# Two rows of a sample per partition in the stores, products in two column tiles, residual inside the matrices

## The chip, the cores and the metric

The kernel runs on one core of a Trainium2 chip. The metric is the device time of one execution in microseconds (us). The core has a matrix engine (TensorE, PE in the profile, with its weight loads listed as PEld), a vector engine (VectorE, DVE), a scalar engine (ScalarE, ACT), GpSimd (POOL) and a sync engine (SyncE, SP). Here ACT and SP only issue transfers, which 16 DMA engines carry out. Matmul results land in a separate memory, PSUM; everything else is in SBUF, a memory of 128 partitions.

## The reference

`x` holds 128 samples of 128 x 1024 f32 values. Each sample has a subject, 0 to 7, and each subject a 128 x 128 matrix. The output is the sample plus the product with its subject's matrix:

```
def _L0_cond_ref(x, subjects, weights):
    w = weights[subjects]
    out = jnp.einsum('bct,bcd->bdt', x, w)
    return out
x = x + _L0_cond_ref(x, itok_B_0_7, L0_cond_weights)
```

The input and the output are 67.11 MB each, the matrices 0.52 MB.

## The kernel before

The 128 samples are worked in `NT` = 32 groups of four. A slot of SBUF holds one group, and there are `SLOTS` = 12 slots. A slot takes the group's input, is added to in place, and is stored from; so a slot is loaded again only when its store has landed (`s_slot`, L222).

**Loads** (`load`, L134, loop at L218) are issued on ACT's queue, one per sample. In DRAM a load reads runs of 16 KB (`ROWS` = 4 rows), in SBUF it writes 4 KB per partition.

**Stores** (`store`, L142, loop at L247) are issued on SP's queue, one per group, and one per two groups for the last 12. SBUF has one row of a sample per partition, so a store writes runs of 4 KB in DRAM. It reads 16 KB runs in SBUF, and 32 KB runs for the last `WHOLE` = 6 groups, where two groups lie next to each other. The first store (L251) is issued in another form, with 4 KB on both sides. From group `EARLY` = 8 on, until the last `LAST` = 8, a store waits until `BEHIND` = 4 more groups have been added (L249).

**Matrices.** The weights arrive over SP's queue (L192) and are sorted by two transposes on DVE and 16 copies on DVE and GpSimd (L208 to L239). For each sample, `place` (L163) copies the subject's matrix from `w_all` to one of four working matrices.

**PE** (`multiply`, L168) runs a loop over the groups in two halves of two samples. A sample takes two matmuls of 512 columns, which the profile records as two each. The two halves of PSUM (`ps`) are filled in turn.

**DVE** (`add`, L183) adds PSUM to the slot in place, half a group per instruction, then places the matrices of the next group.

Semaphores tie them together: GpSimd passes on `s_ready` to PE when a group's loads have landed, `s_go` says that matrices are placed, `s_product` that a half of PSUM is full, `s_added` that a half group is ready for its store. The last store is issued outside the block, after all engines have left it.

Of the kernel before, what the change touches and what calls it, by code (L numbers as in the profile page):

```python
# [25 lines left out]
F32 = mybir.dt.float32  # L26
I32 = mybir.dt.int32
ALU = mybir.AluOpType


G = 2
H = 2

N = 512

SLOTS = 12

P_SLOTS = 2

BEHIND = 4  # L40

EARLY = 8
LAST = 8

PAIR = 2
WHOLE = 6

DMA = 16

SORTED = 18  # L50

IDLE = 3

ROWS = 4

# [25 lines left out]
def kernel(  # L81
# [7 lines left out]
    nc = tc.nc  # L89
    B, C, T = x.shape  # L90
    S, _, D = weights.shape
    NT = B // (G * H)

    def sbuf(name, *shape, dtype=F32):
        return ctx.enter_context(nc.sbuf_tensor(name, list(shape), dtype)).ap()


    room = -(nc.sbuf_base + -nc.sbuf_base % 32) % ALIGN
    if room:
        sbuf("room", C, room // 4)  # L100
    x_all = sbuf("x_all", C, SLOTS * H * G * T)
    xs = [
        x_all[:, i * H * G * T : (i + 1) * H * G * T].rearrange("c (q t) -> c q t", t=T)
        for i in range(SLOTS)
    ]
    w_all = sbuf("w_all", C, S, D)
    w_raw, w_mid, w_late = (xs[SLOTS - 1][:, q, :] for q in range(3))
    ws = [sbuf(f"w{i}", C, 1, D) for i in range(H * G)]
    zeros = sbuf("zeros", C, N)
    given, near, wrap = (sbuf(name, 1, B, dtype=I32) for name in ("given", "near", "wrap"))  # L110
    index = sbuf("index", 1, B + H * G, dtype=I32)
    ps = [
        ctx.enter_context(nc.psum_tensor(f"ps{i}", [D, G, T], F32)).ap() for i in range(P_SLOTS)
    ]
# [4 lines left out]
    s_zeros = tc.alloc_semaphore("s_zeros")  # L119
    s_product = tc.alloc_semaphore("s_product")  # L120
    s_added = tc.alloc_semaphore("s_added")

    s_ready = tc.alloc_semaphore("s_ready")
    s_go = tc.alloc_semaphore("s_go")

    s_slot = [tc.alloc_semaphore(f"s_slot{k}") for k in range(SLOTS)]
    s_head = tc.alloc_semaphore("s_head")
    s_sort = tc.alloc_semaphore("s_sort")

    def emptied(i):  # L130
        turns = i // SLOTS
        return DMA * (H * G + 1) * turns - (DMA * G if i >= SLOTS and i % SLOTS == 0 else 0)

    def load(engine, i, q):  # L134
        transfer(
            nc,
            engine,
            xs[i % SLOTS][:, q, :],
            x[i * H * G + q].rearrange("(a r) t -> a (r t)", r=ROWS),
        ).then_inc(s_head if i * H * G + q < G else s_slot[i % SLOTS], DMA)  # L140

    def store(i, n):  # L142
        at = i % SLOTS * H * G * T
# [9 lines left out]
    def subjects_of(i):  # L153
        _, subject = nc.values_load_multi_w_load_instructions(
            index[0:1, i] if isinstance(i, slice) else index[0:1, bass.ds(i * (H * G), H * G)],
            engines=[mybir.EngineType.DVE],
            min_val=0,
            max_val=S - 1,
            skip_runtime_bounds_check_because="the index is clamped on the chip above",
        )  # L160
        return subject

    def place(h, subject):  # L163
        for q in range(h * G, (h + 1) * G):
            copy = nc.vector.tensor_copy(ws[q], w_all[:, bass.ds(subject[q], 1), :])  # L165
        copy.then_inc(s_go, 1)

    def multiply(slot, h):  # L168
        nc.tensor.wait_ge(s_go, 1).then_inc(s_go, -1)
        nc.tensor.wait_ge(s_ready, 1).then_inc(s_ready, -1)  # L170
        for q in range(h * G, (h + 1) * G):
            for t in range(0, T, N):
                at = slot * (H * G * T) + (q * T + t)
                mm = nc.tensor.matmul(  # L174
                    ps[h][:, q % G, t : t + N],
                    ws[q][:, 0, :],
                    x_all[:, bass.ds(at, N)],
                    start=True,
                    stop=True,
                )  # L180
        mm.then_inc(s_product, 1)

    def add(slot, h):  # L183
        mine = x_all[:, bass.ds(slot * (H * G * T) + h * G * T, G * T)]
        nc.vector.wait_ge(s_product, 1).then_inc(s_product, -1)  # L185
        nc.vector.tensor_tensor(  # L186
            mine, ps[h].rearrange("d g t -> d (g t)"), mine, ALU.add
        ).then_inc(s_added, 1)

    with tc.tile_critical():  # L190

        nc.sync.dma_start(  # L192
            w_raw, weights.rearrange("s (u j) d -> (s u) (j d)", j=S)
        ).then_inc(s_wall, DMA)
        nc.sync.dma_start(given, subjects.rearrange("(o b) -> o b", o=1)).then_inc(s_given, DMA)

        nc.vector.memset(zeros, 0.0).then_inc(s_zeros, 1)  # L197
        nc.tensor.wait_ge(s_zeros, 1)
        for _ in range(IDLE):
            nc.tensor.matmul(  # L200
                ps[P_SLOTS - 1][:, G - 1, :N], zeros[:, :D], zeros, start=True, stop=True
            )

        nc.vector.wait_ge(s_wall, DMA)
        nc.vector.transpose(  # L208
            w_mid.rearrange("p (e h w j) -> p j h e w", e=S, h=4, w=4), w_raw
        ).then_inc(s_sort, 1)  # L210
        nc.vector.memset(index[:, B:], 0).then_inc(s_index, 1)  # L211
        nc.vector.wait_ge(s_given, DMA)
        nc.vector.tensor_scalar(near, given, -S, S - 1, ALU.max, ALU.min).then_inc(s_index, 1)  # L213
        nc.vector.wait_ge(s_index, 2)
        nc.vector.tensor_scalar(wrap, near, 0, S, ALU.is_lt, ALU.mult).then_inc(s_index, 1)  # L215
        nc.vector.wait_ge(s_index, 3)
        nc.vector.tensor_tensor(index[:, :B], near, wrap, ALU.add).then_inc(s_index, 1)  # L217
        for i in range(NT):  # L218
            if i == SLOTS - 1:
                nc.scalar.wait_ge(s_sort, SORTED)  # L220
            if i >= SLOTS:
                nc.scalar.wait_ge(s_slot[i % SLOTS], emptied(i))  # L222
            for q in range(H * G):
                load(nc.scalar, i, q)

        nc.vector.wait_ge(s_sort, 1)
        nc.vector.transpose(w_late, w_mid).then_inc(s_sort, 1)  # L227

        def sort(engine, o, v):
            engine.tensor_copy(  # L230
                w_all[32 * v : 32 * (v + 1), 2 * o : 2 * (o + 1), :],
                w_late[32 * o : 32 * (o + 1)].rearrange("c (e v d) -> c v e d", v=4, d=D)[:, v],
            ).then_inc(s_sort, 1)

        nc.vector.wait_ge(s_sort, 2)
        nc.gpsimd.wait_ge(s_sort, 2)
        for o in range(4):
            for v in range(4):
                sort(nc.gpsimd if v == 3 else nc.vector, o, v)  # L239
        for i in range(NT):  # L240
            if i == 0:
                nc.gpsimd.wait_ge(s_head, DMA * G).then_inc(s_ready, 1)
                nc.gpsimd.wait_ge(s_slot[0], DMA * G).then_inc(s_ready, 1)
            else:
                nc.gpsimd.wait_ge(s_slot[i % SLOTS], emptied(i) + DMA * H * G).then_inc(s_ready, H)

        for i in [*range(NT - SLOTS), *range(NT - SLOTS, NT, PAIR)]:  # L247
            n = 1 if i < NT - SLOTS else PAIR
            nc.sync.wait_ge(s_added, (i + n + (BEHIND if EARLY <= i < NT - LAST else 0)) * H)  # L249
            if i == 0:  # L250
                nc.sync.dma_start(  # L251
                    out[: H * G].rearrange("g d t -> d g t"), xs[0]
                ).then_inc(s_slot[0], DMA)
            elif i + n < NT:
                store(i, n).then_inc(s_slot[i % SLOTS], DMA)


        nc.vector.wait_ge(s_index, 4)
        nc.vector.wait_ge(s_sort, SORTED)
        subject = subjects_of(slice(0, H * G))  # L260
        for h in range(H):
            place(h, subject)
        with nc.vector.Fori(0, NT) as turn:  # L263
            subject = subjects_of(turn + 1)
            for h in range(H):
                add(turn % SLOTS, h)
                place(h, subject)
        with nc.tensor.Fori(0, NT) as turn:
            for h in range(H):
                multiply(turn % SLOTS, h)  # L270

    with tc.tile_critical() as waits:
        for i in range(NT - SLOTS, NT - PAIR, PAIR):
            nc.scalar.wait_ge(s_slot[i % SLOTS], emptied(i + SLOTS))
    last = store(NT - PAIR, PAIR)

    tc.add_manual_dep(
        last.ins,
# [31 lines left out]
```

## Time and profile before

| What | Value |
|---|---|
| Median of 3 runs (lowest to highest) | 323.02 us (322.99 to 323.08) |
| Profiled execution: span of the instructions | 320.9 us |
| Between the span and the runs' median | 2.1 us |
| HBM read, written | 67.63 MB, 67.11 MB |
| Load of one sample, median from issue to landing | 34.2 us |
| Store of one group, median from issue to landing | 18.3 us |
| Store of two groups, median from issue to landing | 30.3 us |

The profile lists for each engine its busy time, and, in 40 equal slices of the span, the busy share of each engine and of the DMA engines. A group row gives line, engine, operation, output and inputs, then the count, the busy time with the mean duration of one, and the idle time before them with what ended it. A queue row gives packets, megabytes and the time that the packets took as a share of 16 engines over the window asked for; q10 carries the loads of x here, and q1 the stores and the matrices. A timeline row gives start, duration, and what was run how often, and in brackets the wait ahead of it.

### The profile page before, as it was taken

The page shows a single profiled execution, that of the slowest core. Times are in us where ns is not written, and L with a number is a line of the kernel's source. Part 1 is how long each engine was busy: PE and PEld are TensorE (multiplying, and loading weights), DVE is VectorE, ACT ScalarE, POOL GpSimd, SP SyncE. Part 2 cuts the span into 40 slices and gives each one's busy share as a digit, 9 for nine tenths or more (in the row PEclk, how much of TensorE's full clock was granted, in tenths as well). Part 3 has the DMA queues.
Part 4 walks back from the last instruction along what each step waited for, and adds up shares of the span by engine and source line. Part 5 has one row for each costly group of instructions (what it writes and reads, how often), then busy time and mean ns, then how long its engine had stood idle before and what let it go on. Part 6 is the DMA issues. An engine that isn't in the chain of part 4 may idle for free. (4 is left out here: it accounts for less than half of the span.)

```text
span 320.9 us, 2386 instructions
## 1 busy us (share of the span) xinstructions
PE 248.9 (78%) x518; PEld 102.8 (32%) x518; DVE 172.6 (54%) x216; POOL 1.9 (1%) x8
## 2 busy tenths in 40 slices
PE   6199999999997699998498469988599957874000
PEld 2134444444433244443133224333244422331000
DVE  4636776777676167775435362675367745066000
POOL 0200000000000000000000000000000000000000
PEclk9679999999999599999789797999799989599555
DMA  7999999999999999999999999999999999999996
GB/s 294 425 425 412 426 423 432 429 423 425 425 425 425 425 424 425 425 429 425 429 435 431 427 427 429 425 425 425 425 425 425 425 425 425 427 427 455 429 445 274
DMA packets 10803, 134.76 MB, mean 420 GB/s; under 512 B 2481, under 2 KB 2482, under 8 KB 3122
## 3 DMA queue, kind: packets, MB, share of 16 engines
q1 hardware_dynamic: 4658, 67.64, 49.7%
q10 hardware_dynamic: 6144, 67.12, 49.6%
q14 instruction: 1, 0.01, 0.0%
HBM read 67.63 MB, written 67.11 MB: 420 GB/s over the span
## 5 line engine op out<-in xcount | busy, mean ns | idle before, releaser
L174 PE MATMUL ps<-x_all,w 128*128 x512 | 243.8, 635 | 42.0 <-PEq L170 34.3
L186 DVE TENSOR_TENSOR x_all<-ps,x_all 128x2048 f32 x64 | 146.7, 2292 | 117.3 <-DVEq L185 117.3
L174 PEld LDWEIGHTS ps<-x_all,w 128*128 128x128 f32 x512 | 100.9, 203 | 185.2 <-issue 184.6
L165 DVE COPY w<-w_all 128x128 f32 x132 | 23.2, 219 | 0.8 <-DVE w_all L230 0.8
L200 PE MATMUL ps<-zeros 128*128 128x512 f32 x6 | 5.2, 1033 | 1.7 <-DVE zeros L197 1.7
L230 DVE COPY w_all<-x_all 32x256 f32<-32x256 f32 x12 | 3.9, 326 | 0.4
L208 DVE STREAM_TRANSPOSE x_all<-x_all 128x1024 f32<-128x1024 f32 x1 | 2.0, 1992 | 3.1 <-DMA x_all<-in_L_cond_weights_dram 3.1
L200 PEld LDWEIGHTS ps<-zeros 128*128 128x128 f32 x6 | 1.8, 328 | 3.7 <-issue 2.1
L230 POOL COPY w_all<-x_all 32x256 f32<-32x256 f32 x4 | 1.7, 425 | 8.3 <-DVE x_all L227 8.1
L227 DVE STREAM_TRANSPOSE x_all<-x_all 128x1024 f32<-128x1024 f32 x1 | 1.2, 1225 | 0.0
L197 DVE MEMSET zeros<- 128x512 f32 x1 | 0.5, 485 | 1.0 <-SPq L190 1.0
L217 DVE CUSTOM_DVE_ANT_0 index<-near,wrap 1x256 uint16<-1x256 uint16 x1 | 0.3, 280 | 0.0
L215 DVE TENSOR_SCALAR wrap<-near 1x128 int32<-1x128 int32 x1 | 0.2, 215 | 0.0
L213 DVE TENSOR_SCALAR near<-given 1x128 int32<-1x128 int32 x1 | 0.2, 205 | 0.0
L297 POOL MEMSET const-bfloat16-1.0<- 128x1 bf16 x1 | 0.1, 100 | 0.0
L297 POOL MEMSET const-float32-0.0<- 128x1 f32 x1 | 0.1, 98 | 0.2 <-issue 0.2
L297 POOL MEMSET const-uint8-127<- 128x1 uint8 x1 | 0.1, 98 | 0.0
L297 POOL MEMSET const-float32-1.0<- 128x1 f32 x1 | 0.1, 97 | 0.0
L297 DVE BASE_LOAD x1 | 0.0, 21 | 0.1
L211 DVE MEMSET index<- 1x4 int32 x1 | 0.1, 62 | 0.0
## 6 DMA issues: line engine op xcount, KB each, us to landing
x_all<-in_x_dram ACTq DMA_DIRECT2D x128, 512.0 KB, 34.2
out_dram<-x_all SPq DMA_DIRECT2D x20, 2048.0 KB, 18.3
out_dram<-x_all SPq DMA_DIRECT2D x6, 4096.0 KB, 30.3
x_all<-in_L_cond_weights_dram SPq DMA_DIRECT2D x1, 512.0 KB, 3.7
given<-in_itok_B_dram SPq DMA_DIRECT2D x1, 0.5 KB
```

The lines of the kernel that those rows point to most:

```text
L165: copy = nc.vector.tensor_copy(ws[q], w_all[:, bass.ds(subject[q], 1), :])
L174: mm = nc.tensor.matmul(ps[h][:, q % G, t : t + N], ws[q][:, 0, :], x_all[:, bass.ds(at, N)], start=True, stop=True,)
L186: nc.vector.tensor_tensor(mine, ps[h].rearrange("d g t -> d (g t)"), mine, ALU.add).then_inc(s_added, 1)
L197: nc.vector.memset(zeros, 0.0).then_inc(s_zeros, 1)
L200: nc.tensor.matmul(ps[P_SLOTS - 1][:, G - 1, :N], zeros[:, :D], zeros, start=True, stop=True)
L208: nc.vector.transpose(w_mid.rearrange("p (e h w j) -> p j h e w", e=S, h=4, w=4), w_raw).then_inc(s_sort, 1)
L213: nc.vector.tensor_scalar(near, given, -S, S - 1, ALU.max, ALU.min).then_inc(s_index, 1)
L215: nc.vector.tensor_scalar(wrap, near, 0, S, ALU.is_lt, ALU.mult).then_inc(s_index, 1)
L217: nc.vector.tensor_tensor(index[:, :B], near, wrap, ALU.add).then_inc(s_index, 1)
L227: nc.vector.transpose(w_late, w_mid).then_inc(s_sort, 1)
L230: engine.tensor_copy(w_all[32 * v : 32 * (v + 1), 2 * o : 2 * (o + 1), :], w_late[32 * o : 32 * (o + 1)].rearrange("c (e v d) -> c v e d", ...
L297: nc = _bacc.Bacc("TRN2", target_bir_lowering=False, num_devices=1)
```

## The change

The stores are given two rows of a sample per partition. A sample's 128 output rows then fill 64 partitions, and two samples lie above each other. In DRAM a store writes runs of 8 KB in place of 4 KB, and it always reads the group, or the two groups, as one run per partition: 16 KB for a group, 32 KB for two. Stores of two groups are made for the last 12 groups as before.

For that, PE makes each product in two parts. The columns of the matrices are sorted beforehand into even and odd ones (`w_all`, L251 of the changed kernel), and each matmul has 64 of them. Two samples write the two halves of the partitions of one bank of PSUM. The number of matmuls doubles, and each has half the width.

Input and output no longer have the same layout, so the slot is split: `IN` = 4 slots of inputs, `OUT` = 8 slots of sums, 12 in all. The residual is no longer added from the slot. The identity is added to each matrix when it is placed, so that the product contains the sample; DVE then only copies PSUM to the output slot. The copy of the second half of a group is split in two, the first bank first, since its end tells that PE has read the group's inputs (`s_eaten`). A load waits for `s_eaten` of the group four before. DVE waits for `s_room`, which GpSimd passes on when the store of eight groups before has landed. `BEHIND` is gone. The matrices are loaded on ACT's queue ahead of x, in runs of 512 B, and sorted by one DVE copy.

```diff
-G = 2
 H = 2
+P = 2
+R = 2
-SLOTS = 12
-BEHIND = 4
-EARLY = 8
-LAST = 8
+IN = 4
+OUT = 8
 PAIR = 2
-WHOLE = 6
+WHOLE = 12
-IDLE = 3
+IDLE = 7
...
     def load(i, q):
+        at = (i % IN * Q + q) * T
...
-            out[i * H * G : (i + n) * H * G].rearrange("g d t -> d g t"),
-            x_all[:, at : at + n * H * G * T].rearrange(
-                "d (o t) -> d o t", o=1 if i >= NT - WHOLE else n
-            ),
+            out[i * Q : (i + n) * Q].rearrange("(g h) (a r) t -> (h a) g (r t)", h=H, r=R),
+            x_out[:, at : at + n * P * SIZE].rearrange("a (o f) -> a o f", o=1),
...
+    def place(u, subject):
+        return [
+            nc.vector.tensor_tensor(
+                ws[u][q], w_all[:, bass.ds(subject[q], 1), :], same, ALU.add
+            )
+            for q in range(Q)
+        ]
...
+        for p in range(P):
+            nc.tensor.wait_ge(s_free, 1).then_inc(s_free, -1)
+            for b in range(BANKS):
+                e, t = divmod(b * N, T)
+                for h in range(H):
+                    q = p * H + h
+                    at = (i % IN * Q + q) * T + t
+                    mm = nc.tensor.matmul(
+                        ps[p][h * A : (h + 1) * A, b],
+                        ws[i % 2][q][:, 0, e * A : (e + 1) * A],
+                        x_in[:, at : at + N],
...
+        transfer(
+            nc,
+            nc.scalar,
+            w_raw.rearrange("c (s d) -> c s d", s=S),
+            weights.rearrange("s c d -> c s d"),
+        ).then_inc(s_wall, DMA)
...
+        for i in range(NT):
+            if i >= IN:
+                nc.scalar.wait_ge(s_eaten, i - IN + 1)
+            for q in range(Q):
+                load(i, q)
...
+            if i - OUT in stored:
+                n, count = stored[i - OUT]
+                nc.gpsimd.wait_ge(s_out[i % OUT], count).then_inc(s_room, n)
+            nc.gpsimd.wait_ge(s_in[i % IN], DMA * Q * (i // IN + 1)).then_inc(s_ready, 1)
...
+        for i, n in stores[:-1]:
+            nc.sync.wait_ge(s_added, i + n)
+            store(i, n).then_inc(s_out[i % OUT], DMA)
...
+                nc.vector.wait_ge(s_room, 1).then_inc(s_room, -1)
+                nc.vector.wait_ge(s_product, 1).then_inc(s_product, -1)
+                copy(slot, 0, 0, BANKS).then_inc(s_free, 1)
+                nc.vector.wait_ge(s_product, 1).then_inc(s_product, -1)
+                copy(slot, 1, 0, 1).then_inc(s_eaten, 1)
+                copy(slot, 1, 1, BANKS).then_inc(s_free, 1)
+                placed = place(u, subject)
+                placed[0].then_inc(s_added, 1)
+                placed[-1].then_inc(s_go, 1)
```

ACT's loads at the start of its program before: 44 loads (11 groups of four) without a wait, one group that waits for the sorted matrices, and then four at a time behind the store that empties their slot.

```order
L67 DMA x_all<-in_x_dram 128x1024 x44
L67 DMA x_all<-in_x_dram 128x1024 [waits s_sort]
L67 DMA x_all<-in_x_dram 128x1024 x3
L67 DMA x_all<-in_x_dram 128x1024 [waits s_slot0]
L67 DMA x_all<-in_x_dram 128x1024 x3
L67 DMA x_all<-in_x_dram 128x1024 [waits s_slot1]
```

The same place of the changed kernel:

```order
L63 DMA x_out<-in_L_cond_weights_dram 128x8x128
L63 DMA x_in<-in_x_dram 128x1024 x16
L63 DMA x_in<-in_x_dram 128x1024 [waits s_eaten]
L63 DMA x_in<-in_x_dram 128x1024 x3
L63 DMA x_in<-in_x_dram 128x1024 [waits s_eaten]
```

The matrices now stand ahead of x on this queue, 16 loads go without a wait in place of 44, and each later group waits for PE to be through with a slot, not for a store.

SP's whole list of transfers before, from the matrices and the subjects to the last store, which is issued outside the block (the row with the many waits is the end of the block):

```order
L192 DMA x_all<-in_L_cond_weights_dram 128x1024
L195 DMA given<-in_itok_B_7_dram 1x128
L251 DMA out_dram<-x_all 128x4x1024 [waits s_added]
L67 DMA out_dram<-x_all 128x4x1024 [waits s_added] x19
L67 DMA out_dram<-x_all 128x8x1024 [waits s_added] x5
L190 NO_OP [waits SP_49,DVE_sequencer_49,PE_sequencer_49,SP_sequencer_49,Activation_sequencer_49,Pool_sequencer_49]
L67 DMA out_dram<-x_all 128x8x1024
```

And of the changed kernel:

```order
L206 DMA given<-in_itok_B_7_dram 1x128
L63 DMA out_dram<-x_out 128x2x2048 [waits s_added] x20
L63 DMA out_dram<-x_out 128x4x2048 [waits s_added] x5
L198 NO_OP [waits SP_49,DVE_sequencer_49,PE_sequencer_49,SP_sequencer_49,Activation_sequencer_49,Pool_sequencer_49]
L63 DMA out_dram<-x_out 128x4x2048
```

The number of stores and their places stay; runs of 1024 values became runs of 2048, the first store has the form of the others, and the matrices have left this queue.

DVE's loop over the groups before, one group (ISA rows compute addresses):

```order
L186 ISA [waits s_product]
L186 TENSOR_TENSOR x_all<-ps,x_all 128x2048
L165 ISA
L165 COPY w<-w_all 128x128
L165 ISA
L165 COPY w<-w_all 128x128
L186 ISA [waits s_product]
L186 TENSOR_TENSOR x_all<-ps,x_all 128x2048
```

The first group of the two that a turn of the changed loop has:

```order
L193 ISA [waits s_room,s_product]
L193 COPY x_out<-ps 128x2048
L193 ISA [waits s_product]
L193 COPY x_out<-ps 128x512
L193 ISA
L193 COPY x_out<-ps 128x1536
L166 ISA
L166 TENSOR_TENSOR w<-w_all,same 128x128
```

The adds became copies, the second one in two parts, a wait for an empty output slot was added, and the matrices of a group are placed behind both halves.

More of the change, by code (lines that the diff above doesn't have):

```diff
@@ L91 @@
     S, _, D = weights.shape
-    NT = B // (G * H)
+    A = D // R
+    Q = P * H
+    NT = B // Q
+    SIZE = R * T
+    BANKS = SIZE // N
     def sbuf(name, *shape, dtype=F32):
         return ctx.enter_context(nc.sbuf_tensor(name, list(shape), dtype)).ap()
+    same = sbuf("same", C, 1, D)
+    index = sbuf("index", 1, B + 2 * Q, dtype=I32)
+    given, near, wrap = (sbuf(name, 1, B, dtype=I32) for name in ("given", "near", "wrap"))
     room = -(nc.sbuf_base + -nc.sbuf_base % 32) % ALIGN
@@ L119, with load @@
     s_zeros = tc.alloc_semaphore("s_zeros")
+    s_same = tc.alloc_semaphore("s_same")
+    s_sort = tc.alloc_semaphore("s_sort")
     s_product = tc.alloc_semaphore("s_product")
+    s_eaten = tc.alloc_semaphore("s_eaten")
     s_added = tc.alloc_semaphore("s_added")
     s_ready = tc.alloc_semaphore("s_ready")
+    s_free = tc.alloc_semaphore("s_free")
     s_go = tc.alloc_semaphore("s_go")
[L126 to L134, printed above, removed]
+    s_room = tc.alloc_semaphore("s_room")
+    s_in = [tc.alloc_semaphore(f"s_in{k}") for k in range(IN)]
+    s_out = [tc.alloc_semaphore(f"s_out{k}") for k in range(OUT)]
+    stores = [(i, 1) for i in range(NT - WHOLE)]
+    stores += [(i, PAIR) for i in range(NT - WHOLE, NT, PAIR)]
+    stored, counts = {}, [0] * OUT
+    for i, n in stores:
+        counts[i % OUT] += DMA
+        stored[i] = (n, counts[i % OUT])
+    def load(i, q):
+        at = (i % IN * Q + q) * T
         transfer(
             nc,
[L137 to L140, printed above, removed]
+            nc.scalar,
+            x_in[:, at : at + T],
+            x[i * Q + q].rearrange("(b r) t -> b (r t)", r=ROWS),
+        ).then_inc(s_in[i % IN], DMA)
     def store(i, n):
-        at = i % SLOTS * H * G * T
+        at = i % OUT * P * SIZE
         return transfer(
@@ L161, in subjects_of, with multiply @@
         return subject
[L163 to L168, printed above, removed]
+    def place(u, subject):
[5 more added lines that the diff above has]
+        ]
+    def multiply(i):
         nc.tensor.wait_ge(s_go, 1).then_inc(s_go, -1)
@@ L170, in multiply @@
         nc.tensor.wait_ge(s_ready, 1).then_inc(s_ready, -1)
[L171 to L188, printed above, removed]
@@ L190 @@
-    with tc.tile_critical():
-        nc.sync.dma_start(
-            w_raw, weights.rearrange("s (u j) d -> (s u) (j d)", j=S)
+        for p in range(P):
[9 more added lines that the diff above has]
+                        x_in[:, at : at + N],
+                        start=True,
+                        stop=True,
+                    )
+            mm.then_inc(s_product, 1)
@@ L194, with copy @@
+    def copy(slot, p, first, last):
+        at = slot * (P * SIZE) + (p * SIZE + first * N)
+        return nc.vector.tensor_copy(
+            x_out[:, bass.ds(at, (last - first) * N)],
+            ps[p][:, first:last].rearrange("d b n -> d (b n)"),
+        )
+    with tc.tile_critical():
+        transfer(
+            nc,
+            nc.scalar,
+            w_raw.rearrange("c (s d) -> c s d", s=S),
+            weights.rearrange("s c d -> c s d"),
         ).then_inc(s_wall, DMA)
@@ L199 @@
         for _ in range(IDLE):
[L200 to L210, printed above, removed]
-        nc.vector.memset(index[:, B:], 0).then_inc(s_index, 1)
+            nc.tensor.matmul(ps[P - 1][:, BANKS - 1], zeros[:, :D], zeros, start=True, stop=True)
+        nc.vector.memset(index[:, B:], 0).then_inc(s_index, 1)
+        nc.gpsimd.wait_ge(s_zeros, 1).then_inc(s_room, OUT)
+        nc.gpsimd.affine_select(
+            same[:, 0, :],
+            zeros[:, :D],
+            [[-1, R], [-R, A]],
+            ALU.not_equal,
+            1.0,
+            base=0,
+            channel_multiplier=1,
+        ).then_inc(s_same, 1)
+        for i in range(NT):
[3 more added lines that the diff above has]
+                load(i, q)
         nc.vector.wait_ge(s_given, DMA)
@@ L218 @@
         for i in range(NT):
[L219 to L224, printed above, removed]
-        nc.vector.wait_ge(s_sort, 1)
[L227 to L258, printed above, removed]
@@ new lines @@
+        nc.vector.wait_ge(s_sort, 1)
+        nc.vector.wait_ge(s_same, 1)
+        for u in range(2):
+            placed = place(u, subject[u * Q : (u + 1) * Q])
+            placed[0].then_inc(s_free, 1)
+            placed[-1].then_inc(s_go, 1)
+        with nc.vector.Fori(0, NT // 2) as turn:
+            for u in range(2):
+                subject = subjects_of(bass.ds(turn * (2 * Q) + (u + 2) * Q, Q))
+                slot = (turn * 2 + u) % OUT
+                nc.vector.wait_ge(s_room, 1).then_inc(s_room, -1)
[6 more added lines that the diff above has]
+                placed[0].then_inc(s_added, 1)
+                placed[-1].then_inc(s_go, 1)
@@ L272 @@
+        with nc.tensor.Fori(0, NT // IN):
+            for i in range(IN):
+                multiply(i)
     with tc.tile_critical() as waits:
-        for i in range(NT - SLOTS, NT - PAIR, PAIR):
-            nc.scalar.wait_ge(s_slot[i % SLOTS], emptied(i + SLOTS))
-    last = store(NT - PAIR, PAIR)
+        for i, n in stores[:-1]:
+            if i >= NT - OUT:
+                nc.scalar.wait_ge(s_out[i % OUT], stored[i][1])
+    last = store(*stores[-1])
     tc.add_manual_dep(
```

40 lines of the change are left out of this document (14 added, 26 removed).

## The prediction

> **What bounds the kernel now.** I read the page's slices first, then its queues, then windows at both ends.
>
> ```profile
> span 320.9 us, 2386 instructions
> PE 248.9 (78%) x518; PEld 102.8 (32%) x518; DVE 172.6 (54%) x216; POOL 1.9 (1%) x8
> DMA  7999999999999999999999999999999999999996
> DMA packets 10803, 134.76 MB, mean 420 GB/s; under 512 B 2481, under 2 KB 2482, under 8 KB 3122
> q1 hardware_dynamic: 4658, 67.64, 49.7%
> q10 hardware_dynamic: 6144, 67.12, 49.6%
> ...
> 2.00:4.00 2.00, 2.00 (x3) 0.84 (x3) 0.00 (x0) 0.00 (x0) 1.00 0.99 315
> 5.00:25.00 20.00, 12.29 (x21) 4.78 (x20) 10.90 (x26) 1.70 (x4) 0.74 1.01 428
> 125.00:185.00 60.00, 47.92 (x100) 19.80 (x99) 32.34 (x39) 0.00 (x0) 0.91 1.00 425
> 303.00:316.00 13.00, 0.00 (x0) 0.00 (x0) 0.00 (x0) 0.00 (x0) 0.50 1.00 426
> 318.60:320.90 2.30, 0.00 (x0) 0.00 (x0) 0.00 (x0) 0.00 (x0) 0.50 0.00 0
> ```
>
> The DMA engines are full in every slice but the first and the last. In the windows (length, busy of PE, PEld, DVE, POOL, clock, DMA share, GB/s) they work from 2.0 us to about 318.5 us without a hole, at 425 to 428 GB/s whether they load, store or do both. 134.76 MB in 316.5 us is 425.8 GB/s. So the time is 2.0 (first issue) + 316.5 (bytes) + 2.4 (end) = 320.9 us, and 2.1 us outside the span make the 323.0 of the runs. PE and DVE have slack. Only two things can move the time: the price of a byte, and a hole in the stream. A group (4 samples) is 2.10 MB in and 2.10 MB out: 4.93 us each way.
>
> Why there is no hole at the end:
>
> ```profile
> q10 hardware_dynamic: 19, 0.05, 3.1%
> ...
> 292.81 2.29 DVE L186 TENSOR_TENSOR x_all<-ps,x_all 128x2048 f32 x1 [0.81 <-DVEq L185]
> 295.02 0.35 DVE L165 COPY w<-w_all 128x128 f32 x2
> 295.69 0.54 SPq L67 DMA_DIRECT2D out_dram<-x_all  x1
> ```
>
> The first row is the loads' queue in 283 to 287 us: its last 19 packets. The loads end at about 283.3, and 35 us of stores are left, about 7 groups: 12 slots and the four groups by which stores are held back let loads run that far ahead. The last add ends at 295.1 and its store is issued at 295.7, 23 us before the queue would run dry. The chain of the last group costs nothing.
>
> **The price of a byte.**
>
> ```profile
> q10 hardware_dynamic: 459, 4.90, 72.5%
> q1 hardware_dynamic: 462, 1.89, 28.7%
> ...
> q1 hardware_dynamic: 1005, 14.63, 57.4%
> q10 hardware_dynamic: 997, 10.85, 42.8%
> ...
> q1 hardware_dynamic: 185, 5.54, 99.8%
> ```
>
> These are queues (packets, MB, share of 16 engines) in 31 to 47 us (the first store, in 4 KB packets), 125 to 185 (16 KB packets both ways) and 303 to 316 (32 KB). A packet, from share x window x 16 over the packets that carry data (MB over their size): 4 KB 0.159 us, 16 KB 0.617, 32 KB 1.23. So joining four 4 KB reads into one saves 0.636 - 0.617 = 0.02 us, about 7 ns a join, and joining 16 to 32 KB about 4 ns. All stores here write 4 KB runs; no row has 8 KB ones. The change joins two pairs of writes in each 16 KB. Bounds: nothing, or 8 to 14 ns in each 617 (1.3 to 2.2% of the stores' 157.5 us, which is 49.7% of 320.9 less the weights), so 0 to 3.4 us. I take 1.5, near the middle. The first group's store goes from 4 KB to 16 KB packets (-0.2 us), six more groups from 16 to 32 KB (-0.1). **Gain 1.8 us, range 0 to 3.7.**
>
> [...]
>
> **Who gets the engines.** In the first two windows the queues moved 462 against 459 and 1005 against 997 packets, semaphore packets included, whatever their size: turns go packet by packet. A store pair in 32 KB runs is 128 data packets and 16 of semaphores; its 144 turns let 144 load packets through, three 512 KB loads (32 + 16 each), 1.57 MB. So a pair (4.19 MB) drains in 5.77/0.4256 = 13.5 us, and loads move at 0.116 MB/us beside it, 27%. Bound on the other side: the 42.8% of the 16 KB window.
>
> **The engines.**
>
> ```profile
> L174 PE MATMUL ps<-x_all,w 128*128 x512 | 243.8, 635 | 42.0 <-PEq L170 34.3
> L186 DVE TENSOR_TENSOR x_all<-ps,x_all 128x2048 f32 x64 | 146.7, 2292 | 117.3 <-DVEq L185 117.3
> L165 DVE COPY w<-w_all 128x128 f32 x132 | 23.2, 219 | 0.8 <-DVE w_all L230 0.8
> 158.26 9.66 PE L174 MATMUL ps<-x_all,w 128*128 x16 [4.53 <-PEq L170]
> 181.01 8.53 PE L174 MATMUL ps<-x_all,w 128*128 x16 [4.54 <-PEq L170]
> 273.78 9.92 PE L174 MATMUL ps<-x_all,w 128*128 x16 [3.35 <-PEq L170]
> 285.44 7.13 PE L174 MATMUL ps<-x_all,w 128*128 x16 [1.74 <-PEq L170]
> 287.26 0.19 PEld L174 LDWEIGHTS ps<-x_all,w 128*128 128x128 f32 x1 [0.24 <-issue]
> 287.69 0.19 PEld L174 LDWEIGHTS ps<-x_all,w 128*128 128x128 f32 x1 [0.24 <-issue]
> ```
>
> PE: a group was 16 matmul records (two for each f32 matmul), one every 0.43 us, 7.1 us; after a wait of 3.35 us or more it took 8.5 to 9.9 at a lower granted clock. Now it is 32 records of 64 columns. Two that follow each other go to different halves of the columns or to the same half in turn. If the halves work beside each other, it is 16 steps of 0.43, still 7.1 us; if not, 32 x 0.43 = 13.7. No row shows half-width matmuls, so both are bounds. [...]
>
> DVE: per group 2.29 for the 128x2048 copy, 0.6 and 1.7 for the two parts of the other (the same rate), 4 x 0.22 for the sums with the identity (nearest row: the copy; twice that if two SBUF inputs cost as two): 5.5, at most 6.4, against 2 x 2.29 + 4 x 0.22 = 5.5 before. Under the 9.85 us that the DMA needs per group, so nothing.
>
> Residual in the matrix: the add's second operand goes, no DMA changes. The four GpSimd copies and twelve DVE copies of the sorted weights go, beside loads that never stop: nothing.
>
> **The start.**
>
> ```profile
> q1 hardware_dynamic: 130, 0.50, 41.8%
> 4.71 1.99 DVE L208 STREAM_TRANSPOSE x_all<-x_all 128x1024 f32<-128x1024 f32 x1 [3.10 <-DMA x_all<-in_L_cond_weights_dram]
> 14.54 80.47 PE L174 MATMUL ps<-x_all,w 128*128 x176 [7.71 <-DVE w L165]
> 26.95 0.42 SPq L251 DMA_DIRECT2D out_dram<-x_all  x1
> q1 hardware_dynamic: 6, 0.02, 6.0%
> ```
>
> The first row is the weights in 0 to 4 us: 0.418 x 4 = 1.7 us. Now they come as 1024 runs of 512 B. At the join price above a run is 0.019 + 0.007 us, 64 per engine 1.7 us: nothing; if each cost as much as a 4 KB packet, 10.2 us, 8.5 more. I take the first, as the fixed part is what the joins show. They stand ahead of x on ACT's queue, and the 16 loads behind them last to 2.0 + 1.7 + 19.7 = 23.4 us. The 17th waits for group 0 to be eaten, and all later loads stand behind it on ACT. Weights at 4.7, a strided copy of 128x1024 (2.0, as the transposing row), four sums (0.9): PE starts by 9, not 14.5, and group 0 is eaten by 17 (24 at the low clock). Before 23.4, so no hole; at the low clock a hole of 1 to 2 us.
>
> Under load a store starts late: issued at 26.95, its first six packets fall in 30 to 31 us (last row): 3.5 us. At the idle start issue to data is 1.1.
>
> **The tail, the term that decides.** Loads may now run only 4 groups ahead of PE (a load waits for the eaten slot, not the stored one), nothing holds stores back, and their bigger packets win turns. So stores keep up with PE, PE waits for loads, and little is left when the loads end. Worked for the last pairs: two groups take 19.7 us, 13.5 beside a pair and 6.2 with loads alone (2.62 MB). From group 29's landing to the first packet of pair (28, 29): 0.2 + 7.1 (PE) + 2.6 (copies, first sum) + 0.1 + 3.5 = 13.5 us. In it, loads move 2.62 MB alone and 7.3 x 0.116 = 0.85 beside the pair ahead: 3.47 of the 4.19 MB of groups 30 and 31. The rest, 0.72 MB, takes 6.2 us beside the pair. Then 4.19 - 6.2 x 0.31 = 2.27 MB of the pair are left, 5.3 us. PE had waited 2.2 us for group 31, so it is at full clock: 0.2 + 7.1 + 3.5 (copies, four sums, issue, 3.1 before) + 1.1 = 11.9 us until the last pair moves. **Hole 11.9 - 5.3 = 6.6 us.** Its bounds: the pair has only just begun when the loads end (9.9 left): 2.0; nothing is left and PE is at the low clock (9.9): 14.7.
>
> Sum on the profiled execution: 320.9 - 1.8 + 6.6 = 325.7, with 2.1 outside the span **327.8 us**.
>
> **Rivals.**
> A, the half-width matmuls run one after the other: 13.7 x 32 + 9 + 3.5 + 1.1 + 9.9 + 2.4 + 2.1 = 466 us. For it: no row shows halves side by side. Against it: only that they share nothing but rows.
> B, weight loads stop hiding. The rows at 287.26 and 287.69 show loads of 0.19 us under matmuls 0.43 apart, with the same 128 rows. If each step had to show one of half width (0.1) to a full one (0.19), a group is 8.5 to 9.9 us: the tail grows by 1.4 to 2.8, to 329 to 331, and at 9.9 PE is the bound: 32 x 9.9 + 28 = 345. [...]
> C, the other side: the tail stays covered. If the pair (26, 27) still stands ahead of (28, 29) when the loads end, more than 11.9 us (5.1 MB) is left, the chain is hidden, and 323.0 - 1.8 = 321.2. For it: 3.5 us from issue to data delays stores. Against: stores win 57 to 73% of turns, so that a backlog drains. From 11.9 us left it decides; between 10 and 11.9 the two cancel.
> D, 8 KB writes cost what 4 KB ones do: 329.6, in the range.
>
> **How the numbers follow.** Forecast with its bounds (D in it) 0.69, A 0.10, B 0.08, C 0.13. The range is from C's 321.2 and the least hole with the full gain (323.0 - 3.7 + 2.0 = 321.3) to no gain with a hole of 12 (335); A, and the ends beyond, are left out. A measurement here tells 0.2% (0.65 us) from no change. Faster: C (0.13) and 0.03 of the forecast, where the least hole meets the full gain, 0.16; the same 0.07, also from its small holes; slower 0.59 of it with A and B, 0.77.
>
> **What would show it.** Gain: a store packet of 16 KB under 0.617 us, of 32 KB under 1.23. Tail: a slice with an idle DMA some 12 to 20 us before the end, loads ending at about 300 instead of 283. Engines: 32 records in 7.1 us. Wrong if the DMA row has no hole, or if PE is busy through the span.

## The result and the profile after

| | Before | After |
|---|---|---|
| Median of the runs (lowest to highest) | 323.05 us (322.99 to 323.26) | 331.62 us (329.84 to 334.19) |
| Ratio, 95% interval | | 1.027 (1.022 to 1.032) |
| Span of the profiled execution | 320.9 us | 328.1 us |

The change is slower by 2.7%, and its runs spread over 4 us where those of before stay within 0.3 us. The profiled execution is the fastest of its runs (329.8 us). In the experiments below two runs lie far above the others of their kernel, 330.06 us in a10 and 641.37 us in a3, and their cause is not known; the medians and ranges leave them out.

The page of the changed kernel: span, the busy tenths of the DMA engines with what they moved, the two queues (q10 now carries the matrices too), and the groups of matmuls and copies.

```profile
span 328.1 us, 3169 instructions
DMA  6999999999999999999999999999999999999947
GB/s 250 422 430 387 424 434 428 430 428 424 436 424 430 430 424 434 424 431 426 428 432 426 428 428 430 432 424 448 416 420 445 398 428 420 382 352 434 444 200 320
q10 hardware_dynamic: 7184, 67.64, 49.9%
q1 hardware_dynamic: 3746, 67.11, 47.8%
...
L182 PE MATMUL ps<-x_in,w 128*64 128x512 f32 x1024 | 241.8, 632 | 60.6 <-PEq L176 58.0
L182 PEld LDWEIGHTS ps<-x_in,w 128*64 128x64 f32 x1024 | 87.5, 146 | 214.9 <-issue 214.9
L193 DVE COPY x_out<-ps 128x2048 f32 (+2 forms) x96 | 148.7, 1577 | 133.0 <-DVEq L266 98.6
L166 DVE TENSOR_TENSOR w<-w_all,same 128x128 f32<-128x128 f32 x136 | 30.1, 284 | 0.1
```

The last but one slice, 312 to 320 us, moves 200 GB/s: that is the hole before the last pair of stores. Twice as many matmul records as before take the same busy time (241.8 us against 243.8), and DVE was busy 178.1 us of the span against 172.6: neither engine is the bound. The holes by windows (a row is the window's start and end, its length, the busy time of PE, PEld, DVE and POOL, the granted clock, the DMA share and GB/s):

```profile
2.00:4.00 2.00, 2.00 (x3) 0.84 (x3) 0.71 (x3) 0.22 (x1) 1.00 0.45 121
...
22.00:26.00 4.00, 4.00 (x21) 1.57 (x19) 2.73 (x2) 0.00 (x0) 1.00 1.06 360
...
284.00:291.00 7.00, 7.00 (x36) 2.57 (x34) 5.58 (x8) 0.00 (x0) 1.00 0.92 286
291.00:303.00 12.00, 12.00 (x60) 4.29 (x58) 10.24 (x14) 0.00 (x0) 1.00 1.05 451
303.00:312.00 9.00, 8.03 (x38) 2.70 (x34) 5.56 (x8) 0.00 (x0) 1.00 0.94 405
312.00:317.00 5.00, 0.00 (x0) 0.00 (x0) 3.16 (x6) 0.00 (x0) 0.85 0.27 118
```

Against 426 GB/s the loss is length x (1 - GB/s / 426): 3.6 us in 312 to 317 and 0.4 in 303 to 312; 2.3 in 284 to 291, of which the next window returns 0.7 (451 GB/s at a share of 1.05: the profile puts a packet down to where it starts); 0.6 in 22 to 26; and 0.9 more than before in 2 to 4 (121 against 315 GB/s). That is 7.1 us. (A window can lose bytes while its DMA share stays near 1, as 22 to 26 does: its packets then took longer, 0.77 us for 16 KB against 0.62 in 12 to 20.) Stores took 47.8% of 328.1 us, 156.8; before it was 159.5 less 1.7 for the matrices, 157.8: 1.0 us back. The sum, 6.1, is most of the 7.2 by which the span grew; the last 1.1 us I cannot place.

The end of PE's work, DVE's last sums and SP's last issue (a row is start, duration, operation and count; in brackets the wait ahead):

```profile
243.80 7.09 PE L182 MATMUL ps<-x_in,w 128*64 128x512 f32 x32 [1.04 <-PEq L176]
259.60 9.39 PE L182 MATMUL ps<-x_in,w 128*64 128x512 f32 x32 [8.71 <-PEq L176]
274.65 29.29 PE L182 MATMUL ps<-x_in,w 128*64 128x512 f32 x128 [5.67 <-PEq L176]
304.85 7.09 PE L182 MATMUL ps<-x_in,w 128*64 128x512 f32 x32 [0.91 <-PEq L176]
...
314.45 0.89 DVE L166 TENSOR_TENSOR w<-w_all,same 128x128 f32<-128x128 f32 x4
315.64 0.54 SPq L63 DMA_DIRECT2D out_dram<-x_out  x1
```

While a pair of stores drains, PE starves: waits of 8.71 and 5.67 us. Then no store is at hand (one pair is issued at 253.7 us, the next at 286.2), loads run alone and fill the four slots, and PE is behind with four groups in a row (29.3 us), in which loads stop for want of a slot: the dip at 284 to 291. PE ends at 311.9, DVE at 315.3, and the last pair is issued at 315.6 into an empty DMA.

### The profile page after: what moved, and what is told of

The parts are those of the page before. It is cut to its first block, busy times and chain, and to the rows that moved or that the text cites. A ratio compares the mean times of both kernels' runs of the same rounds, so it can differ in the third digit from the quotient of the medians.

```text
span 328.1 us, 3169 instructions
## 1 busy us (share of the span) xinstructions
PE 249.6 (76%) x1038; PEld 90.7 (28%) x1038; DVE 178.1 (54%) x239; POOL 0.5 (0%) x5
## 3 DMA queue, kind: packets, MB, share of 16 engines
q1 hardware_dynamic: 3746, 67.11, 47.8%
## 5 line engine op out<-in xcount | busy, mean ns | idle before, releaser
L182 PE MATMUL ps<-x_in,w 128*64 128x512 f32 x1024 | 241.8, 632 | 60.6 <-PEq L176 58.0
L193 DVE COPY x_out<-ps 128x2048 f32 (+2 forms) x96 | 148.7, 1577 | 133.0 <-DVEq L266 98.6
L182 PEld LDWEIGHTS ps<-x_in,w 128*64 128x64 f32 x1024 | 87.5, 146 | 214.9 <-issue 214.9
L166 DVE TENSOR_TENSOR w<-w_all,same 128x128 f32<-128x128 f32 x136 | 30.1, 284 | 0.1
L211 PE MATMUL ps<-zeros 128*128 128x512 f32 x14 | 7.8, 721 | 1.7 <-DVE zeros L208 1.7
L211 PEld LDWEIGHTS ps<-zeros 128*128 128x128 f32 x14 | 3.2, 239 | 5.5 <-issue 3.8
L251 DVE COPY w_all<-x_out 128x1024 f32<-128x1024 f32 x1 | 0.7, 694 | 2.4 <-DMA x_out<-in_L_cond_weights_dram 2.4
```

Source lines behind the costliest of these rows:

```text
L166: nc.vector.tensor_tensor(ws[u][q], w_all[:, bass.ds(subject[q], 1), :], same, ALU.add)
L182: mm = nc.tensor.matmul(ps[p][h * A : (h + 1) * A, b], ws[i % 2][q][:, 0, e * A : (e + 1) * A], x_in[:, at : at + N], start=True, stop=True,)
L193: return nc.vector.tensor_copy(x_out[:, bass.ds(at, (last - first) * N)], ps[p][:, first:last].rearrange("d b n -> d (b n)"),)
L211: nc.tensor.matmul(ps[P - 1][:, BANKS - 1], zeros[:, :D], zeros, start=True, stop=True)
L251: nc.vector.tensor_copy(w_all.rearrange("c s (r a) -> c s r a", r=R), w_raw.rearrange("c (s a r) -> c s r a", s=S, r=R),).then_inc(s_sort, 1)
```

## The experiments

Each ratio is to runs of the kernel before on the same chip. It compares means without the profiled run, so it can differ a little from the ratio of the medians. First come the four combinations of the two suspects in the stores, pairs and the missing hold-back.

**a1_singles.** Every store for one group.

```diff
-WHOLE = 12
+WHOLE = 0
```

> The changed kernel with every store for one group (no pairs, so 16 KB packets to the end). Theory (turns go packet by packet, so pairs in 32 KB packets take 73% of the DMA, starve PE of loads, and leave no stores for the tail): loads keep 43% beside a store, PE is starved less, and the last store is 4.9 us long, not 9.9; 325 to 328 us, and no wait of PE over 5 us after 240 us. Rival (the tail hole comes from the dropped hold-back alone, pairs do not matter): still 330 to 334. Rival (PE or the half-width matmuls are at fault): 331, unchanged.

Measured: 328.47 us (327.92 to 331.34), ratio 1.020 (1.017 to 1.023), a little over the 325 to 328 of my theory and 3.2 us under the changed kernel, with ranges that overlap (327.92 to 331.34 against 329.84 to 334.19). The end in windows:

```profile
300.00:309.00 9.00, 7.54 (x36) 2.82 (x34) 7.58 (x10) 0.00 (x0) 1.00 1.01 429
309.00:315.00 6.00, 5.87 (x28) 2.08 (x24) 3.01 (x5) 0.00 (x0) 1.00 0.86 366
315.00:320.00 5.00, 0.00 (x0) 0.00 (x0) 3.16 (x6) 0.00 (x0) 0.84 0.14 59
```

PE's longest wait after 240 us is 4.7 us now, as I had expected, but the DMA still idles for most of 315 to 320. So pairs are at most a part of the loss.

**a10_pairs_hold2.** Pairs kept; a hold-back of two groups put back.

```diff
+BEHIND = 2
+EARLY = 8
+LAST = 4
-            nc.sync.wait_ge(s_added, i + n)
+            nc.sync.wait_ge(s_added, i + n + (BEHIND if EARLY <= i < NT - LAST else 0))
```

> The changed kernel with pairs and 32 KB packets kept, and the hold-back of two groups of a3 (from group 8 to 27). It fills the square of pairs or singles, hold-back or none: changed kernel 331.6, a1 (singles) 328.5, a3 (singles, hold of two) 325.2. If the two parts simply add: 331.6 - 3.3 = 328.3. If pairs spend what was held back, as in a2 (theory): 330 to 340.

Measured: 324.84 us (324.33 to 326.27), 1.008 (1.006 to 1.010), 6.8 us under the changed kernel. My theory gave 330 to 340: it fell. It is also below the 328.3 of simple adding. With held stores the pairs do no harm that can be told (a3, with singles, has 324.98 us).

```profile
261.73 29.36 PE L185 MATMUL ps<-x_in,w 128*64 128x512 f32 x128 [11.22 <-PEq L179]
295.00 8.78 PE L185 MATMUL ps<-x_in,w 128*64 128x512 f32 x32 [3.92 <-PEq L179]
307.49 0.54 SPq L66 DMA_DIRECT2D out_dram<-x_out  x1
...
300.00:318.50 18.50, 3.79 (x18) 1.21 (x14) 5.45 (x7) 0.00 (x0) 0.66 0.99 427
318.50:320.00 1.50, 0.00 (x0) 0.00 (x0) 0.00 (x0) 0.00 (x0) 0.50 0.21 87
```

The last store is issued at 307.5 into a DMA that stays full (427 GB/s) to 318.5. That is what the tail lacked.

**a3_singles_hold2.** Both edits.

> Both: every store for one group, and a hold-back of two groups from group 8 to 27. Theory: two groups more are unstored when the loads end, 4.2 MB or 9.9 us, about as long as the last group's chain (11.9), and turns stay near 57 to 43; the hole shrinks to 0 to 2 us: 321.2 to 323.5. If the four input slots are the limit by themselves: over 325.

Measured: 324.98 us (324.75 to 327.54), 1.008 (1.006 to 1.011). My theory's 321.2 to 323.5 was missed, and this is at the edge of what I had given to the rival (over 325). The hold-back buys 3.5 us with singles and 6.8 with pairs; both edits together buy no more than the hold-back with pairs. What is left, 2.0 us over before, shows at least in part in its first window and its last ones:

```profile
2.00:4.00 2.00, 2.00 (x3) 0.84 (x3) 0.71 (x3) 0.21 (x1) 1.00 0.56 152
...
310.00:318.50 8.50, 0.00 (x0) 0.00 (x0) 2.67 (x6) 0.00 (x0) 0.68 0.99 424
318.50:320.00 1.50, 0.00 (x0) 0.00 (x0) 0.00 (x0) 0.00 (x0) 0.50 0.46 197
320.00:322.00 2.00, 0.00 (x0) 0.00 (x0) 0.00 (x0) 0.00 (x0) 0.50 0.06 25
```

The stream is full to 318.5, but a few packets still move in 320 to 322 us. Before the change the DMA was all but empty from 318.6. Beside its 128 data packets a store has 16 under 512 B, which I take for its completions (4610 packets on q1 are 32 x 144 and 2); those of the last store lie at 319.0 to 321.7 us here and at 318.8 to 319.6 before the change.

**a2_hold4 and a11_hold2_ends_early.** The changed kernel with a hold-back of four groups that ends at group 23, as before the change, and with one of two that ends there.

```diff
+BEHIND = 4
+EARLY = 8
+LAST = 8
...
```

> The changed kernel with the old hold-back put back (a store waits for four more groups from group 8 to 23), pairs kept. Rival theory (the dropped hold-back is the cause): the hole closes, 321.5 to 323. Theory (pairs drain what was held back faster than loads come, and four input slots make loads stop while stores are held): no gain, 329 to 336, with the hole before the last pair still there.

Measured: 339.66 us (337.02 to 341.96), 1.049 (1.044 to 1.054): slower still, and beyond the 329 to 336 of my theory. (The diff leaves out the line with the wait, which is that of a10.)

```profile
112.00:134.00 22.00, 22.00 (x106) 8.36 (x104) 17.32 (x23) 0.00 (x0) 1.00 0.86 290
...
316.00:329.00 13.00, 7.71 (x30) 2.31 (x27) 5.45 (x7) 0.00 (x0) 0.89 0.16 69
```

It loses twice. In 112 to 134 four stores are held and PE is busy throughout, so that loads wait for their four slots: 290 GB/s. In 316 to 329 the tail lies bare, 69 GB/s. For a11 (`LAST` = 8 in a10, nothing else):

> The kernel of a10_pairs_hold2 with the hold-back of two groups ending at group 23 in place of 27. a2 (a hold of four, ending at 23) was 8 us slower than the changed kernel, a10 (two, ending at 27) 6 us faster; they differ in two things. If the end of the hold is what counts (stores released at 24 drain ahead of the loads, and nothing waits when the loads end): 329 to 335, near the changed kernel. If only its size did the harm in a2 (four held groups fill the output slots): 325.5, as a10.

Measured: 335.0 us (332.09 to 336.99), 1.039 (1.034 to 1.044). The one number costs 10.2 us against a10, so the end of the hold decides:

```profile
263.36 9.59 PE L185 MATMUL ps<-x_in,w 128*64 128x512 f32 x32 [11.29 <-PEq L179]
...
291.68 22.52 PE L185 MATMUL ps<-x_in,w 128*64 128x512 f32 x96 [4.51 <-PEq L179]
...
312.00:318.00 6.00, 2.20 (x12) 0.54 (x7) 4.52 (x7) 0.00 (x0) 1.00 0.20 87
```

PE's long wait, 11.3 us, is no difference: a10 has one of 11.2. What differs is what is left for the end. In a11 two pairs are issued at 245.7 and 246.3 us, one behind the other; in a10 the second of them waits until 273.3. In a11 PE then works on its last three groups from 291.7 to 314.2, the loads end near 302, and from 294 us on no store moves until the last pair but one is issued at 303.3. In a10 that pair is issued at 287.6, behind pairs at 273.3 and 287.0. Holding to group 27 covers the tail.

**b1_nohold.** The kernel before, without its hold-back.

```diff
-BEHIND = 4
+BEHIND = 0
```

> The kernel before, with its hold-back of four groups set to none; nothing else. Theory (what matters is how many groups are computed and not stored when the loads end): stores win 57% of the turns, loads lose their lead of 7 groups, and the last group's chain shows: a hole of 3 to 7 us, 325 to 330. Rival (the twelve shared slots alone keep loads ahead, the loss of the change is its four input slots): 323, unchanged.

Measured: 328.38 us (327.83 to 331.83), 1.020 (1.016 to 1.024). As the theory said, and the rival's 323 is out. One number, and the kernel before, with its twelve shared slots, loses 5.5 us:

```profile
300.00:310.00 10.00, 10.00 (x24) 4.38 (x24) 7.42 (x8) 0.00 (x0) 1.00 0.98 421
310.00:315.20 5.20, 0.82 (x2) 0.00 (x0) 2.81 (x5) 0.00 (x0) 1.00 0.12 50
```

**a5_in8.** Eight slots of inputs, four of sums.

```diff
-IN = 4
-OUT = 8
+IN = 8
+OUT = 4
```

> The changed kernel with 8 slots of inputs and 4 of sums in place of 4 and 8. Rival (four input slots are too few): the hole closes, 321.5 to 324. Theory (a lead in inputs is spent by PE at once; only sums that wait for their store cover the tail, and there are fewer slots for them): no gain, 328 to 336.

Measured: 332.17 us (330.77 to 333.22), 1.027 (1.025 to 1.029), the changed kernel's time. More room for inputs, taken from the room for sums, buys nothing: the DMA idles in two places. (More room for inputs with eight slots of sums kept was not tried.)

```profile
299.00:306.00 7.00, 7.00 (x35) 2.77 (x32) 5.59 (x8) 0.00 (x0) 1.00 0.26 112
306.00:315.00 9.00, 9.00 (x44) 3.46 (x40) 7.08 (x8) 0.00 (x0) 1.00 0.95 408
315.00:320.50 5.50, 0.33 (x2) 0.00 (x0) 3.16 (x6) 0.00 (x0) 1.00 0.22 95
```

**a4_runs4k.** a3 with 4 KB runs in DRAM, the old address pattern (rows of the output land elsewhere in their group).

```diff
-            out[i * Q : (i + n) * Q].rearrange("(g h) (a r) t -> (h a) g (r t)", h=H, r=R),
+            out[i * Q : (i + n) * Q].rearrange("g d t -> d g t"),
```

> The kernel of a3_singles_hold2 with stores that write runs of 4 KB, as before the change (rows of the output land at other places of the same group; bytes, packets read and everything else are equal). It prices the 8 KB runs alone. From packets of 0.612 against 0.616 us in the two profiles: 4096 x 0.0035 / 16 = 0.9 us slower than a3. By the forecast's 1.5: 1.5 slower. If run length in DRAM costs nothing: equal within 0.2.

Measured: 325.22 us (324.77 to 326.38), 1.007 (1.006 to 1.008); a3 has 324.98. The pages, first a3's span and stores' queue, then a4's:

```profile
span 323.2 us, 3179 instructions
q1 hardware_dynamic: 4610, 67.11, 48.6%
...
span 324.6 us, 3179 instructions
q1 hardware_dynamic: 4610, 67.11, 48.7%
```

Packets took 157.1 us with 8 KB runs and 158.1 with 4 KB: 1.0 us, as the 0.9 worked out from the profiles. In the time nothing of it can be told: the medians lie 0.24 us apart, inside the spread of either. Where the 1.0 us of packet time goes is not shown.

**a6_halves_apart.** The order of the matmuls: eight records for one half of the columns, then eight for the other.

```diff
-            for b in range(BANKS):
-                e, t = divmod(b * N, T)
-                for h in range(H):
+            for h in range(H):
+                for b in range(BANKS):
+                    e, t = divmod(b * N, T)
```

> The changed kernel with the loops over banks and halves exchanged: eight records of one half of the columns follow each other, then eight of the other. It asks what makes 32 half-width records fit in 7.1 us. If neighbours in different halves run beside each other and records start in order: they now run one after the other, 13.7 us for a group, PE is busy to the end, about 466 us. If PE looks far enough ahead to pair them anyway, or a half-width record costs half: 7.1 us for a group and about 331.

Measured, one run: 331.9 us.

```profile
81.72 8.94 PE L182 MATMUL ps<-x_in,w 128*64 128x512 f32 x32 [2.25 <-PEq L176]
...
81.70:83.40 1.70, 1.68 (x4) 0.59 (x5) 1.17 (x5) 0.00 (x0) 1.00 1.02 434
83.40:85.20 1.80, 1.80 (x9) 0.72 (x8) 0.00 (x0) 0.00 (x0) 1.00 1.00 428
```

A group takes 8.94 us against 7.09 with halves in turn, and not 13.7. The two windows at its start show how: four records run in the first 1.7 us, by the kernel's order all of the first half and 0.43 us apart, and nine in the next 1.8 us, 0.20 us apart, when the second half has joined in. So a half-width record did not cost half here (0.43 us, as at full width), and the halves do run beside each other, not only as neighbours. The 1.9 us a group do not reach the end: the one run lies inside the range of the changed kernel.

**a7_hold3_late, a8_split, a9_split_late** were tries to win back the last 2 us of a3: three groups held late (20 to 25) and the matrices loaded behind two samples; the last group's store in two halves, the first issued when its half is copied; the same with the hold only from group 20. First a7 against a3, then a8 (and a9 with `EARLY` = 20).

```diff
-BEHIND = 2
-EARLY = 8
-LAST = 4
+BEHIND = 3
+EARLY = 20
+LAST = 6
...
+                if i == 0 and q == 1:
+                    transfer(
+                        nc,
+                        nc.scalar,
+                        w_raw.rearrange("c (s d) -> c s d", s=S),
+                        weights.rearrange("s c d -> c s d"),
+                    ).then_inc(s_wall, DMA)
```

```diff
+        nc.sync.wait_ge(s_eaten, NT)
+        half(NT - 1, 0).then_inc(s_half, DMA)
...
-    last = store(*stores[-1])
+    last = half(NT - 1, 1)
```

> The kernel of a3_singles_hold2 with a hold-back of three groups, only from group 20 to 25, and the matrices' load moved behind the first two samples on the same queue. Theory: the late hold leaves one group more for the tail (4.9 us), which closes what a3 still had there (2.2 us), and a start with 16 KB packets saves 0.5 of the 0.9 us that the DMA idles in 2 to 4 us: 322 to 323.5. If three held groups stop the loads as four did in a2: over 325.

> The kernel of a3_singles_hold2 with the last group's store cut in two halves, the first issued as soon as its half is copied (some 2.5 us earlier than the whole). Theory (a3 still loses about 2 us because the last group's chain is a little longer than what is left to store): 322.5 to 324. If a3's loss is spread over the whole run: 325, unchanged.

> The kernel of a8_split with the hold-back only from group 20 to 27. Theory: only the sums that wait when the loads end count, so the early hold buys nothing: as a8_split within 0.7 us. If the hold's early part keeps a lead that a late one cannot build any more: 1 to 3 us slower than a8_split.

Measured: 326.00 us (324.32 to 326.76), 326.39 (324.38 to 326.86) and 324.97 (324.65 to 326.21), ratios 1.008, 1.009 and 1.006. None beats a3 by more than the spread: the theories for a7 (322 to 323.5) and a8 (322.5 to 324) were missed, and a9, expected within 0.7 us of a8 or slower, is 1.4 faster. The chain of the last group is not what a3 still loses. One loss is new. The slowest windows of a8, a9 and a7, in this order:

```profile
116.00:119.00 3.00, 3.00 (x16) 1.21 (x14) 1.93 (x3) 0.00 (x0) 1.00 0.84 218
...
233.00:236.00 3.00, 3.00 (x18) 1.08 (x16) 1.93 (x3) 0.00 (x0) 1.00 0.92 262
...
239.00:242.00 3.00, 3.00 (x18) 1.21 (x16) 1.93 (x2) 0.00 (x0) 1.00 0.88 191
```

Each lies where its hold-back begins. In a9 no store is issued between 200.8 and 230.8 us, in a8 none between 83.9 and 113.9; PE is busy throughout, and as in a2 the loads run alone until their four slots are full. With the windows beside them this loses 1.6 us in a8, 1.3 in a9 and 3.1 in a7. a4's profile has such a dip too (262 GB/s in 116 to 119 us), those of a3 and a10 have none. The profiled runs with it are among the slower of their kernels (326.13, 326.04, 326.76 and, in a4, 326.38 us); that the faster ones, from 324.3 us, go without it is likely and not shown. So the start of a hold has a price too. a9's end:

```profile
300.00:318.00 18.00, 7.09 (x32) 2.65 (x32) 7.94 (x13) 0.00 (x0) 0.81 1.00 425
318.00:320.30 2.30, 0.00 (x0) 0.00 (x0) 0.00 (x0) 0.00 (x0) 0.50 1.01 427
320.30:323.00 2.70, 0.00 (x0) 0.00 (x0) 0.00 (x0) 0.00 (x0) 0.50 0.12 49
```

Full to 320.3, and then 49 GB/s until the last packets: the 16 completions of the last store lie at 320.3 to 322.8 us. In a10 they lie at 318.4 to 321.1. Where a hole came shortly ahead they lie close together: 326.5 to 326.7 in the changed kernel, 324.9 to 325.0 in b1. Why they lie up to 2.7 us apart without such a hole, and only 0.8 in the kernel before, stays open; so does whether the early part of a hold is worth anything. No version beat the kernel before.

## Why the prediction was right, and where not

**The bound: right.** The time is the bytes, the two ends and the holes; matmuls that are slower by a quarter (a6: 8.94 us a group against 7.09, and 331.9 us in its one run) change nothing that can be told.

**The tail: right in kind, too large in size.** I had 6.6 us from one hole before the last pair. The profile has 4.0 there (303 to 317), 2.6 less, and 1.6 at 284 to 291 which I did not see: I let loads go on at all times, but after a pair they fill the four slots and stop. The chain also ran differently: not a PE that waits for the last load (it waits 0.9 us, and takes 7.09 for the group at a granted clock of 1.00), but one that still works off what loads brought all at once. That dropping the hold-back is the cause was argued; a10 (-6.8 us) and b1 (+5.5 us) show it. Its old numbers would not have done: a2 has them and is slower by 8 us.

**The turns: right.** The queues in 230 to 240 us of the changed kernel, the first pair beside loads:

```profile
q1 hardware_dynamic: 97, 3.18, 74.3%
q10 hardware_dynamic: 101, 1.11, 26.4%
```

97 packets against 101, and 74% of the time for the stores, where I had worked out 73. Over the longer 231 to 271 us it is 68%. But what follows from it depends on what is held: with stores held to the end, pairs cost nothing that can be told (a10 324.84 us, a3 324.98).

**The price of a byte: mis-sized.** I had a gain of 1.8 us, 1.5 of it for the 8 KB runs. The stores' packets took 1.0 us less, and a4 gives 1.0 for the 8 KB runs alone, none of which the medians tell. So D, that 8 KB writes cost what 4 KB ones do, is out for the packets and open for the time. Two slips in the working move nothing: 49.7% of 320.9 less the weights is 157.8, not 157.5, and the join of 16 to 32 KB comes to 6 ns, not 4, before rounding.

**The start: wrong.** I had no loss. The runs of 512 B move 121 GB/s in 2 to 4 us, 0.9 us lost. In a7, where the matrices stand behind two samples, 2 to 4 us moves 352 GB/s and 4 to 6 us only 204: the loss goes with them and is not saved. And I worked out 3.5 us from issue to data under load, but left them out of the 17th load. DVE's copies of the second half of group 0, and the mean of the first of them (692 ns, by forms):

```profile
18.69 2.36 DVE L193 COPY x_out<-ps 128x512 f32 x2 [1.05 <-DVEq L268]
...
L193 DVE COPY x_out<-ps 128x512 f32 x32 | 22.1, 692 | 34.4 <-DVEq L268 34.4
```

So the group is eaten at 19.4, and its successor's data 3.5 us later would come at 22.9, near the 0.6 us lost in 22 to 26. But the loads still move 451 GB/s in 22 to 24 us, and fall to 270 in 24 to 26 with the engines busy (share 1.02), so the dip is no plain wait for late data. Its cause is not shown.

**The engines: right.** The 7.1 us that the sum has for a group were an estimate, 16 steps of 0.43 us; no run before the change shows half-width matmuls. Measured: 32 records take 7.09 us at a granted clock of 1.00, 0.22 us apart on the mean. DVE was busy 178.1 us, 5.6 a group, where I had 5.5 to 6.4. Rival A is out, and so is B: 32 weight loads of 146 ns on top of 16 steps of 0.43 us would make 11.6 us a group, not 7.09; in the group at 304.85 us the 32 loads, all of 128 rows, are busy for 2.62 us within its 7.09.

**C, the covered tail: out.** Loads ended at 303, and PE's chain lay bare.

Sum: forecast 327.8, measured 331.6; the profiled run's 328.1 against 325.7. The missing 2.4 us are the start (1.5), the dip at 284 to 291 (1.6) and the smaller gain (0.8), less a smaller last hole (2.6), and 1.1 that I cannot place. That they come so near is in part luck: a hole that was too large stood in for losses that I had put at nothing. The other 1.4 us: the median lies 1.8 above this profile's run, the fastest, and 0.4 less than forecast lies outside its span.

## What to carry to other kernels

Where transfers bound a kernel, count at the moment the loads end what is computed and not yet stored: it must last longer than the chain of the last tile (35 us of stores were left before the change, and no hole came; after it the stores ran out, and the hole was 4.0 us). A hold-back that looks like a delay builds that stock, and it must reach to the last tiles (324.8 us when it ends at group 27, 335.0 at 23); here room for more inputs, taken from the sums, did not replace it (332.2 us). Look at its start too: where the input slots filled while stores were held, the stream dipped to 191 to 290 GB/s (a2, a7, a8, a9). A saving of 1.0 us in the price of bytes is lost in one hole of 4.0.

## What the hardware showed unexpectedly

Two half-width matmul streams with separate columns ran beside each other even when eight records of one half stood ahead of the first of the other (8.94 us a group, against 7.09 with neighbours paired and 13.7 by the estimate for one after the other). I had expected records to start in order. And without a hole shortly ahead, the completions of the last store came up to 2.7 us apart (a3, a10), against 0.2 us behind a hole (the changed kernel).
